# A list-scheduled megakernel: side work of the first mixer held behind its filter groups, and the end of an inverse moved one phase on

## The chip, the cores and the metric

The kernel is one program on one core of a Trainium2 chip. The core has five engines with queues of their own: TensorE (PE: matmuls, and PEld: its weight loads), VectorE (DVE), ScalarE (ACT), GpSimd (POOL) and SyncE (SP, which here only issues DMAs; ACT issues some as well). The metric is the device time of one execution in microseconds, lower is better. The kernel before took 4566.36 us (median of three runs, 4564.21 to 4567.75).

## What is computed

Eight sequences of 512 tokens with 256 channels go through four layers, each a mixer and a feed-forward part, all in float32: `x = x + layernorm(f(layernorm(x)))`, eight times. Only the first mixer matters here:

```python
q, k, v = silu(short_conv(x @ W.T))                  # 4 heads of 64
delta_out = delta_rule_chunkwise(q, k, v, beta)      # chunks: T = inverse(I - A), then a scan
local_s, local_m, local_l = fir(v, 3), fir(v, 15), fir(v, 63)
probs = softmax(logits / temp) * (1 - 5 * eps) + eps
o = (probs[0] * local_s + probs[1] * local_m + probs[2] * local_l
     + probs[3] * delta_out + probs[4] * v)
out = rmsnorm(o, norm_w) @ Wo.T
```

The reference uses chunks of 32 tokens; the kernel inverts 64 x 64 blocks, as two 32 x 32 ones and what lies between them.

## The kernel before

The program is written with a tile framework. Its planner orders the instructions of each engine itself: among those that it takes to be ready it issues the one written first. An instruction that it takes to be ready early can so land far ahead of work that was written before it. Once ordered, each engine's queue runs in that order. Pools of tiles that follow one another share an area of on-chip memory; what touches a later pool first waits for the earlier ones' last uses.

The function `l0_attn` has three phases:

1. **Front** (0 to about 241 us of the profile): `front(b)` for each of the 8 sequences: transposes, projections, short convolutions on DVE (L457), transposed values into `Vw`, products k k^T into `S`, all but `Vw` stored to DRAM (`S` to `l0s` at L506 and L510). After the fourth sequence `strengths(0)` and the DVE part of `inverse(0)` run between the steps.
2. **Filters** (248 to about 396 us): 32 groups g of 8 channels. `filters(g)` multiplies `Vw` with Toeplitz matrices `toep` (16 matmuls, L625) into one of 6 PSUM tiles, two per group; DVE multiplies by the gates `gt` into `pr` (L630; 2 buffers); POOL adds four terms to two (`s1`, L636, 1 buffer) and two to one (`s2`, L638, 2 buffers); ACT issues two stores of `s2` to `l0f` (L640). Three `toep` buffers are filled by two SP loads each (L542, L545), three groups ahead. Beside it, written between the groups: `gates(h)` (DVE with one ACT exponential, before g = 0 and at g = 4, 12, 20), `value_scales` (g = 2, an rsqrt on DVE), `scaled_v(b)` (every fourth group, L610, stored by ACT at L613), `query_scales` (g = 22), `strengths(1)` (g = 4), the end of `inverse(0)` with `load_tt` for two sequences (g = 1) and `inverse(1)` (g = 6 to 24, one step per group, its end as the last).
3. **Last phase** (419 to about 701 us): generators `back(b)`, two or three alive at a time and a new one every 16 steps, each some 32 us after the one before. `loads(b)` reads what phases 1 and 2 stored, one sequence ahead; at the end `load_x` reads the residual and `project_out` adds the result to it.

`inverse(g)` handles four sequences in half of the residual buffer `XA` (`X` in the profile): it loads 2 MB of `S` from DRAM (L331) and two small tiles, scales (L343), eliminates 30 columns on DVE (L351, L354), scales again (L357). Its end is `affine_select` on POOL (L360), a diagonal copy (L363), a 2 MB store by SP (L364), and four times a transposing ACT copy into one of two `tt` buffers (L367) with a 512 KB store issued by ACT (L368). `load_tt(b)` reads those blocks back, for sequences 0 and 1 into `XA`, after two POOL memsets (L398, L399). `inverse(0)` writes `XA` for sequences 0 to 3, `inverse(1)` for 4 to 7.

The order in which phase 2 is written ends so:

```python
if g == 6:
    inv = inverse(1)
if 6 <= g < 26:
    next(inv, None)
if g == 26:
    for _ in inv:
        pass
```

Of the kernel before, what the change touches and what calls it, by code (L numbers as in the profile page):

```python
# [19 lines left out]
P = 128  # L20
# [254 lines left out]
def l0_attn(K):  # L275
# [6 lines left out]
    with ExitStack() as es:  # L282
# [45 lines left out]
        def inverse(g):  # L328
# [42 lines left out]
            yield  # L371
# [35 lines left out]
        with ExitStack() as e1:  # L407
# [117 lines left out]
            with ExitStack() as ef:  # L525
# [4 lines left out]
                NB_T = 3  # L530
                toep = []
# [17 lines left out]
                rw_all = p1.tile([P, 24, 64], F32, name="rw_all")  # L549
                for r in range(2):  # L550
                    nc.sync.dma_start(
                        out=rw_all[64 * r:64 * r + 64].rearrange("p r t -> p (r t)"),
                        in_=rows_d[:, 256:28 * 64])
# [4 lines left out]
                def wide(name, n=256):  # L558
                    return p1.tile([P, n], F32, name="w" + name)
                gz = rw_all[:, 0:20, :].rearrange("p (h f) t -> p h f t", h=H)  # L560
                gm = wide("gm").rearrange("p (h t) -> p h t", h=H)
                gt = p1.tile([P, H, 4, 64], F32, name="gt")
# [23 lines left out]
                def query_scales():  # L586
                    ssq = wide("ssq")
# [28 lines left out]
                def filters(g):  # L616
# [18 lines left out]
                    s1 = p1.tile([P, 4, 2, 64], F32, tag="s1", name=f"s1_{g}")  # L635
# [9 lines left out]
                for g in range(G):  # L645
                    filters(g)
                    if g % 8 == 4 and g < 24:
                        gates(g // 8 + 1)
                    if g == 2:
                        value_scales()  # L650
                    if g == 22:
                        query_scales()
                    if g % 4 == 3:
                        scaled_v(g // 4)
                    if g == 1:
                        for _ in inv:
                            pass
                        for b in range(2):
                            load_tt(b)
                    if g == 4:  # L660
                        strengths(1, p1)
                    if g == 6:
                        inv = inverse(1)
                    if 6 <= g < 26:
                        next(inv, None)
                    if g == 26:
                        for _ in inv:
                            pass
# [62 lines left out]
        def back(b, TT, TS, qT, kT, V, F):  # L731
# [128 lines left out]
            K.load_x(K.i["x"], [b])  # L860
# [20 lines left out]
        live, done, begun, steps = [back(0, *ahead[0])], 0, 1, 0  # L881
        while live:
            for x in list(live):
                if next(x, x) is x:
                    live.remove(x)
            steps += 1
            if begun < NB and steps >= 16:
                live.append(back(begun, *ahead[begun]))
                begun, steps = begun + 1, 0
                if begun < NB:  # L890
                    ahead[begun] = loads(begun)
# [1739 lines left out]
```

## Time and profile before

The profiled execution took 4566.32 us, its span 4564.6 us.

| stretch of the span, us | what | length | PE busy | DVE busy | ACT busy | POOL busy |
|---|---|---|---|---|---|---|
| 201.0 to 241.0 | end of the front | 40.00 | 32.50 | 17.85 | 28.39 | 8.35 |
| 241.0 to 248.4 | until the last `S` store has landed | 7.40 | 0.00 | 0.00 | 0.66 | 0.00 |
| 248.4 to 395.9 | filters, to the end of the last `pr` | 147.50 | 120.86 | 128.23 | 6.79 | 80.69 |
| 395.9 to 411.4 | to the end of the last `s2` | 15.50 | 0.00 | 0.00 | 5.65 | 3.51 |
| 411.4 to 419.3 | to the first matmul of the last phase | 7.90 | 0.00 | 0.00 | 0.00 | 7.71 |
| 484.5 to 517.0 | one period of the last phase | 32.50 | 30.05 | 21.46 | 12.36 | 7.67 |

Busy times are of one engine each and overlap. "L360" is a line of the kernel; names are the program's tiles without their numbers. A queue such as SPq is the sequencer that issues DMAs: its rows are issues, and a transfer goes on after it. "A <- B: t" in a table of waits says that A stood idle for t until B released it. The end of `inverse(0)` is in the profile at 201.8 to 224.5 us, that of `inverse(1)` at 386.1 to 404.5 us.

### The profile page before, as it was taken

The numbers are of one execution on the slowest core, as the hardware profiler recorded it, in microseconds if no ns is written. First come the engines' busy times: TensorE is split into PE (matmuls) and PEld (weight loads), VectorE is DVE, ScalarE is ACT, GpSimd is POOL, SyncE is SP. The second block draws the span as 40 slices with busy tenths as digits, with TensorE's granted clock in tenths as the row PEclk, the third lists the DMA queues.
The fourth block names the chain that finished last, engine by engine and source line by source line (L and its number), as shares of the span: only waits on it lengthen the run. The fifth ranks groups of instructions, "written<-read, shape, count | busy, mean of one in ns | idle before, by whom it ended". The sixth has DMA issues, their size and how long they took to land. (4 is left out here: it accounts for less than half of the span.)

```text
span 4564.6 us, 63271 instructions
## 1 busy us (share of the span) xinstructions
PE 3962.3 (87%) x21672; PEld 2630.5 (58%) x21672; DVE 2697.3 (59%) x7151; ACT 1982.4 (43%) x4082; POOL 2123.0 (47%) x2079
## 2 busy tenths in 40 slices
PE   8876988999998599789999978898888876899997
PEld 3434775555655399644454544565655544678884
DVE  7775656456747611255566534888888899721115
ACT  5511333444344233334444444767676655311112
POOL 0044222444344244345555423889888879223321
PEclk9987998999999799889999988899999886899999
DMA  4477611000000199500000002344333434337653
GB/s 116 123 208 216 147 48 62 3 8 6 7 5 20 52 251 252 147 5 10 6 6 6 1 23 63 122 127 128 123 119 126 124 109 137 104 115 233 228 181 113
DMA packets 389361, 442.89 MB, mean 97 GB/s; under 512 B 147469, under 2 KB 271487, under 8 KB 388527
## 3 DMA queue, kind: packets, MB, share of 16 engines
q1 hardware_dynamic: 361087, 390.18, 28.6%
q0 software_dynamic: 16272, 31.87, 2.6%
q10 hardware_dynamic: 11680, 16.80, 1.1%
q8 instruction: 172, 2.82, 0.3%
q14 instruction: 150, 1.23, 0.1%
HBM read 372.49 MB, written 66.26 MB: 96 GB/s over the span
## 5 line engine op out<-in xcount | busy, mean ns | idle before, releaser
L2046 POOL TENSOR_TENSOR h<-h,C 128x1024 f32<-128x1024 f32 x256 | 614.0, 2412 | 134.8 <-DVE h L2042 92.9
L2042 DVE TENSOR_TENSOR_SCAN h<-dA,dB 128x512 f32<-128x512 f32 x480 | 568.3, 1209 | 90.9 <-ACT dA L2030 75.2
L1000 POOL TENSOR_SCALAR p<-p,rs 128x128 f32<-128x128 f32 (+3 forms) x256 | 276.6, 1089 | 418.1 <-DVE rs L999 258.9
L2030 ACT ACTIVATE dA<-dl,A 128x512 f32<-128x512 f32 x480 | 330.5, 690 | 174.4 <-DVE h L2042 173.7
L1566 DVE CUSTOM_DVE_ANT_0 junk<-S,mask 128x256 f32<-128x256 f32 (+3 forms) x512 | 249.5, 487 | 194.1 <-PE S L1560 155.8
L2059 PE MATMUL y<-C,h 128*128 128x128 f32 x2048 | 296.3, 296 | 68.4 <-POOL h L2046 68.2
L2059 PEld LDWEIGHTS y<-C,h 128*128 128x128 f32 x2048 | 261.9, 154 | 154.0 <-POOL h L2046 97.6
L1594 ACT ACTIVATE PT<-T 128x128 f32<-128x128 f32 (+3 forms) x512 | 198.2, 435 | 277.9 <-PE T L1589 273.9
L1560 PE MATMUL S<-KZ,QT 64*128 64x512 f32 (+3 forms) x1024 | 259.7, 490 | 23.6 <-DVE mx L1566 23.1
L2258 PE MATMUL gb<-xbT,w_b 128*128 128x256 f32 (+1 forms) x1472 | 255.3, 332 | 1.0 <-ACT ts L2462 0.6
L2258 PEld LDWEIGHTS gb<-xbT,w_b 128*128 128x128 f32 x1472 | 230.2, 191 | 23.1 <-ACT ts L2462 0.8
L2264 DVE TENSOR_TENSOR hTb<-sb,gb 128x512 f32<-128x512 f32 x71 | 48.8, 688 | 325.4 <-PE gb L2258 325.4
L1844 PE MATMUL pf<-fT,w_l_ffn 128*128 128x512 f32 x384 | 208.3, 681 | 30.1 <-ACT fT L1838 10.5
L2025 POOL TENSOR_TENSOR dB<-du,B 128x1024 f32<-128x1024 f32 x96 | 234.0, 2438 | 0.1
L1589 PE MATMUL T<-QT,KZ 64*128 64x384 f32 (+3 forms) x1024 | 216.7, 464 | 2.9 <-ACT PT L1594 2.5
L2025 DVE TENSOR_TENSOR dB<-du,pb 128x1024 f32<-128x1024 f32 x160 | 191.2, 1195 | 23.2 <-ACT pb L2023 21.3
L182 POOL TENSOR_TENSOR X<-X,yn 128x256 f32<-128x256 f32 (+1 forms) x56 | 79.5, 1439 | 257.1 <-ACT yn L177 227.1
L1334 ACT ACTIVATE hT<-h,w_l_ffn 128x128 f32<-128x128 f32 x384 | 109.8, 368 | 196.6 <-PE h L1329 196.6
L1329 PE MATMUL h<-xgT,w 128*128 128x128 f32 x1536 | 184.1, 278 | 0.0
L1597 POOL TENSOR_SCALAR_AFFINE_SELECT PT<-PT 128x512 f32<-128x512 f32 x128 | 81.5, 637 | 218.8 <-ACT PT L1594 206.0
L1560 PEld LDWEIGHTS S<-KZ,QT 64*128 64x128 f32 x1024 | 116.4, 192 | 114.1 <-issue 57.9
L2495 POOL DMA_INDIRECT ys<-yb,place x71 | 70.0, 986 | 238.5 <-ACT yb L2494 224.3
(601 smaller groups left out, 9238.1 us busy)
## 6 DMA issues: line engine op xcount, KB each, us to landing
w_b<-l3f_w SPq DMA_DIRECT2D x138, 512.0 KB
C<-xdd SPq DMA_DIRECT2D x256, 256.0 KB
B<-xdd SPq DMA_DIRECT2D x256, 256.0 KB
w<-l1f_w SPq DMA_DIRECT2D x48, 1024.0 KB
w<-l1f_w SPq DMA_DIRECT2D x48, 256.0 KB
toep<-l0fd SPq DMA_DIRECT2D x32, 320.0 KB
X<-x SPq DMA_DIRECT2D x16, 512.0 KB
toep<-l0fd SPq DMA_DIRECT2D x32, 256.0 KB
```

Of the source, the lines that this page charges most:

```text
L1000: nc.gpsimd.tensor_scalar(p[:, 0:n], p[:, 0:n], rs, None, ALU.mult)
L1560: nc.tensor.matmul(ps[:, 0:n], lhsT=QT[half, qt * P:n], rhs=KZ[half, j % 2, 0:n], start=True, stop=True)
L1566: nc.vector.tensor_tensor_reduce(out=junk[:, 0:n], in0=ps[:, 0:n], in1=mask[:, L - n:L], scale=1.0, scalar=-3.0e38, op0=ALU.add, op1=ALU.m ...
L1589: nc.tensor.matmul(ps[:, 0:n], lhsT=KZ[half, j % 2, kt * P:(kt + 1) * P], rhs=QT[half, kt * P:L], start=True, stop=True)
L1594: nc.scalar.activation(PT[:, j, :], ps[:, 0:n], AF.Exp)
L1844: nc.tensor.matmul(ps, lhsT=gu[:, k, j * 768 + c * P:j * 768 + (c + 1) * P], rhs=R[b]["fT"][:, k, :], start=(k == 0), stop=(k == 1))
L2025: on.tensor_tensor(dBs[k], R[b]["du", h], B[:, None, :].to_broadcast([P, 2, L]), ALU.mult)
L2030: nc.scalar.activation(dA, R[b]["dl", h][:, c, :], AF.Exp, scale=A[:, 2 * h + c, n:n + 1])
L2042: nc.vector.tensor_tensor_scan(hs[k][:, c, :], dA, dBs[k][:, c, :], 0.0, ALU.mult, ALU.add)
L2046: nc.gpsimd.tensor_tensor(hs[k], hs[k], row_C.pop(k)[:, None, :].to_broadcast([P, 2, L]), ALU.mult)
L2059: nc.tensor.matmul(R[b]["y", h][q // 2][:, q % 2, c * P:(c + 1) * P], lhsT=t[:, c, q * P:(q + 1) * P], rhs=K.ident, is_transpose=True, sta ...
L2258: nc.tensor.matmul(ps[:, q, :], lhsT=ww[:, k, (c + q) * P:(c + q + 1) * P], rhs=xT[:, k, :], start=(k == 0), stop=(k == 1))
```

## The change

- The yield at the end of `inverse` moves into the loop over q, so that each of the four copies with its store is a step of its own.
- `behind()` is new: what is written inside it on SP, DVE, ACT or POOL is queued behind the instruction written last on that engine (an edge of order, no wait for its end). All side work of group g stands in such a block after `filters(g)`.
- `inverse(1)` now takes one step at g >= 6 until its DVE part is through (18 steps, g = 23). Its end goes to the last phase: one step at every odd step of the second batch, each in a `behind()`. An assertion says that it is through before the fifth sequence's loads.
- `load_x` in `back` stands in a `behind()`.
- The tiles `s1`, `gt`, `gm`, `ssq` and `rw_all` are made before the `toep` tiles, in that order, and the load of `rw_all` is written before the `toep` memsets. `s1` is one tile instead of one per group from a single buffer.

```diff
@@ inverse(g)
                 nc.scalar.dma_start(
                     out=tt_d[g * P:(g + 1) * P, 1024 * q:1024 * q + 1024],
                     in_=tt.rearrange("p i j -> p (i j)"))
-            yield
+                yield
+
+        @contextmanager
+        def behind():
+
+            with ExitStack() as stack:
+                traced = nc.cur_bb.bb.instructions
+                for e in (mybir.EngineType.SP, mybir.EngineType.DVE,
+                          mybir.EngineType.Activation, mybir.EngineType.Pool):
+                    stack.enter_context(tc.issue_after(
+                        next(x for x in reversed(traced) if x.engine == e)))
+                yield
@@ filters
                 NB_T = 3
+                s1s = p1.tile([P, 4, 2, 64], F32, name="s1")
+                gt = p1.tile([P, H, 4, 64], F32, name="gt")
+                gm = p1.tile([P, 256], F32, name="wgm").rearrange("p (h t) -> p h t", h=H)
+                ssq = p1.tile([P, 256], F32, name="wssq")
+                rw_all = p1.tile([P, 24, 64], F32, name="rw_all")
+                for r in range(2):
+                    nc.sync.dma_start(
+                        out=rw_all[64 * r:64 * r + 64].rearrange("p r t -> p (r t)"),
+                        in_=rows_d[:, 256:28 * 64])
                 toep = []
...
-                    s1 = p1.tile([P, 4, 2, 64], F32, tag="s1", name=f"s1_{g}")
+                    s1 = s1s
...
                 for g in range(G):
                     filters(g)
-                    if g % 8 == 4 and g < 24:
-                        gates(g // 8 + 1)
...
+                    with behind():
+                        if g % 8 == 4 and g < 24:
+                            gates(g // 8 + 1)
+                        if g == 2:
+                            value_scales()
+                        if g == 22:
+                            query_scales()
+                        if g % 4 == 3:
+                            scaled_v(g // 4)
+                        if g == 1:
+                            for _ in inv:
+                                pass
+                            for b in range(2):
+                                load_tt(b)
+                        if g == 4:
+                            strengths(1, p1)
+                        if g == 6:
+                            inv, inverted = inverse(1), False
+                        if g >= 6:
+                            inverted = inverted or next(inv)
+                assert inverted
@@ back(b), and the loop of the last phase
-            K.load_x(K.i["x"], [b])
+            with behind():
+                K.load_x(K.i["x"], [b])
...
             steps += 1
+            if begun == 2 and steps % 2:
+                with behind():
+                    next(inv, None)
             if begun < NB and steps >= 16:
                 live.append(back(begun, *ahead[begun]))
                 begun, steps = begun + 1, 0
+                assert begun < HALF or next(inv, 0) == 0
                 if begun < NB:
                     ahead[begun] = loads(begun)
```

More of the change, by code (lines that the diff above doesn't have):

```diff
@@ L1 @@
 import math
-from contextlib import ExitStack
+from contextlib import ExitStack, contextmanager
 from itertools import chain
@@ L547, in load_toep @@
                         in_=window(fd, 3 * g * 1536 + 384, (8, 80), (1536, 2), (1, 512)))
[L549 to L553, printed above, removed]
                 for g in range(NB_T):
                     load_toep(g)
-                def wide(name, n=256):
-                    return p1.tile([P, n], F32, name="w" + name)
                 gz = rw_all[:, 0:20, :].rearrange("p (h f) t -> p h f t", h=H)
-                gm = wide("gm").rearrange("p (h t) -> p h t", h=H)
-                gt = p1.tile([P, H, 4, 64], F32, name="gt")
                 def gates(h):
@@ L586, in query_scales @@
                 def query_scales():
-                    ssq = wide("ssq")
                     nc.vector.tensor_scalar(
@@ L646, in l0_attn @@
                     filters(g)
-                    if g % 8 == 4 and g < 24:
-                        gates(g // 8 + 1)
[L649 to L668, printed above, removed]
+                    with behind():
[19 more added lines that the diff above has]
+                assert inverted
         p1, p2 = pool(es, "ba", 1), pool(es, "bb", 2)
@@ L880, in l0_attn @@
         ahead = {b: loads(b) for b in range(2)}
-        live, done, begun, steps = [back(0, *ahead[0])], 0, 1, 0
+        live, begun, steps = [back(0, *ahead[0])], 1, 0
         while live:
```

## The prediction

> **What bounds the kernel now.** Only the first mixer is touched, and it ends at about 701 us of a span of 4564.6 us, so I read that stretch alone. First the busy table by stretches (columns: length, then PE, PEld, DVE, ACT, POOL busy with counts, granted clock, DMA share, GB/s):
>
> ```profile
> 241.00:248.40 7.40, 0.00 (x0) 0.00 (x0) 0.00 (x0) 0.66 (x2) 0.00 (x0) 0.63 0.77 137
> 248.40:274.77 26.37, 11.93 (x48) 5.32 (x48) 21.12 (x43) 2.53 (x4) 5.52 (x3) 0.65 0.90 290
> 274.77:395.90 121.13, 108.93 (x464) 53.17 (x464) 107.11 (x171) 4.26 (x4) 75.17 (x63) 0.95 0.63 191
> 248.40:395.90 147.50, 120.86 (x512) 58.49 (x512) 128.23 (x212) 6.79 (x8) 80.69 (x66) 0.89 0.68 209
> 395.90:411.40 15.50, 0.00 (x0) 0.00 (x0) 0.00 (x0) 5.65 (x4) 3.51 (x4) 0.50 0.87 299
> 411.40:419.30 7.90, 0.00 (x1) 0.03 (x2) 0.00 (x0) 0.00 (x0) 7.71 (x15) 0.50 0.82 210
> ...
> 484.50:517.00 32.50, 30.05 (x394) 23.72 (x393) 21.46 (x61) 12.36 (x27) 7.67 (x4) 1.00 0.57 133
> ```
>
> The projections (front) end near 241, the filter loop runs from 248.4 to the last gated product at 395.9, the last phase starts at 419.3. In the loop DVE (128.23) is loaded more than PE (120.86): DVE is its floor. Between 395.9 and 419.3 PE does nothing. The last phase is nearly full of PE (30.05 of 32.50).
>
> Second, the waits of 240 to 420 (us in total, times, longest):
>
> ```profile
> PE pW L740 <- DMA TS<-l0s: 28.4, 1, 28.4
> ...
> PE pf L625 <- DMA l0v<-vs: 20.9, 1, 20.9
> ...
> POOL toep L534 <- DMA l0s<-S: 20.0, 1, 20.0
> POOL s L638 <- DMA l0f<-s: 16.6, 5, 6.3
> DVE rky L90 <- DMA l0s<-S: 12.3, 1, 12.3
> ```
>
> Third, the timeline, for what stands in each queue at the two idle places:
>
> ```profile
> 246.64 0.34 SPq L331 DMA_DIRECT2D X<-l0s  x1
> 248.35 1.13 SPq L551 DMA_DIRECT2D rw_all<-l0rows  x2
> 248.50 5.52 POOL L534 MEMSET toep<- 128x2048 f32 x3 [20.04 <-DMA l0s<-S]
> 248.85 1.53 DVE L90 TENSOR_SCALAR rky<-SSK 128x128 int32<-128x128 int32 x1 [12.27 <-DMA l0s<-S]
> ...
> 274.77 2.47 DVE L630 TENSOR_TENSOR pr<-pf,gt 128x512 f32<-128x512 f32 x4
> ```
>
> ```profile
> 386.06 4.07 POOL L360 TENSOR_SCALAR_AFFINE_SELECT X<-X 128x4096 f32<-128x4096 f32 x1
> ...
> 392.59 3.82 ACT L367 COPY tt<-X 128x1024 f32<-128x1024 f32 x2 [92.09 <-POOL X L363]
> ...
> 400.21 1.91 ACT L367 COPY tt<-X 128x1024 f32<-128x1024 f32 x1 [3.80 <-DMA l0tt<-tt]
> ...
> 404.49 2.11 SPq L74 DMA_DIRECT2D X<-x  x3
> ...
> 410.64 0.72 POOL L638 TENSOR_TENSOR s<-s 128x256 f32<-128x256 f32 x1 [6.27 <-DMA l0f<-s]
> ```
>
> At the head, side work runs before the filters that were written first: the 2 MB load X<-l0s, the rsqrt of value_scales and five scaled_v. So the first product `pr` comes at 274.77, though the loop's memory was free at 248.4. At the tail the end of inverse(1) stands in ACT's queue: copies that wait for their own stores, with the stores f<-s behind them. POOL's last s2 waits for those and ends at 411.36; only then is the loop's memory free for the last phase.
>
> **The change part by part.** The profiled execution took 4566.32 us (span 4564.6 and 1.7 around it); the median of the three runs is 4566.36, so one sum serves both. Against it:
>
> (a) The end of inverse(0) leaves the front. There it cost POOL 4.07 + 0.29 and four memsets of 0.95, ACT four copies of about 1.95 with four DMA issues, SP five issues, and 5 MB (2 MB t, 2 MB tt, 1 MB read back). PE was busy 32.50 us of 201 to 241. At the 94% of 100 to 150 us (46.92 of 50) the same work takes 34.6, which would save 5.4; the other end is 0, as the last front has no next one beside it. I take 3, and 1 more for the stores of S, which land at 248.4 with less traffic beside them. **-4.0** (0 to -6).
>
> (b) The loop. Behind-edges put gates(0) first on DVE. Loop memory frees at 244.4. rw_all (768 KB) and the first filter load (576 KB) take 1.34 MB / 290 GB/s = 4.6 us. One gates is 24.4 / 4 = 6.1 us of DVE by its rows, with an ACT table load of 1.28. So the first `pr` is at about +12 (the two gates in the trace took 265.59 to 274.79, 9.2, which would make it +13.8). What DVE then still has to do is all of 128.23 less gates(0) 6.1 and three filter copies 1.3: 120.8, at 95% busy (47.1 of 50 in 340 to 390) 127 us. PE, starting at about +7 (a memset of 1.9, then the loads) with 32 groups of 16 x 0.235 = 3.76, needs 120 and is done earlier. 12 + 127 = 139.
>
> (c) What the loop newly holds: the end of inverse(0) at g=1 with its 5 MB and its POOL, ACT and SP instructions, and X<-l0s at g=6 instead of ahead. Behind a late copy on ACT stand the f stores, behind those POOL's s2, s1, and then DVE's `pr`; behind a late issue on SP stand the filter loads that PE waits for. The nearest row is the same work at the tail, where POOL stood 16.6 us for f stores. Three groups of PSUM (3 x 3.76 = 11.3) lie between PE and DVE, two `pr` buffers before POOL, so I take 16.6 - 11.3 = 5. The ends are 0 (cover whole) and 34 (the whole chain as the front ran it, 201.8 to 236). The loop becomes 144 against 147.5: **-3.5** (-14 to +26: DVE at 100% and no stall, or the 34).
>
> In bytes: the loop moved 147.5 us x 209 GB/s = 30.8 MB; with 5 more in 144 us it is 249 GB/s, under the 290 seen at a share of 0.90. The Trainium skill, "DMA: Bandwidth & Descriptors", section "Issuing engines are not separate DMA queues", speaks against the change: transfers of SP and of ACT run on the same 16 engines and interleave, so ACT's tt stores delay SP's filter loads. If all 5 MB went ahead of the loads, at the page's roughly 358 GB/s (estimate) that is 14 us in place of my 5, and the total 9 us higher; the trace's share of 0.63 in the loop says that most of it fits beside.
>
> (d) Tail. From the last `pr` to the last s2 were 15.5 us; without copies ahead of the f stores it is s1 1.27 + s2 0.73 + hand-overs, 2.7 as at 275.5 to 278.2. **-12.8** (-13 to -6). New here: scaled_v(7) is held behind group 31, DVE 1.22 and a 512 KB store that must land before TS may be loaded: **+1.5** (0 to 4).
>
> (e) Start of the last phase, 7.9 us now. Three X<-x loads (1.5 MB, 5.3 us at 299 GB/s) no longer stand before it, partly drained by 411.4: **-2.5** (-5 to 0). They come back as one each behind the loads of their batch, as for the other batches now (issued 457.46, needed by POOL at 476.29): free, while those 18 us cover them.
>
> (f) The end of inverse(1) enters the last phase: POOL 4.4 in a gap of 11.2 before its next work, free; SP one issue; 4 MB where the share is 0.57, more than one 32.5 us period has free but with loads issued a period ahead, free if that holds; ACT four copies, 7.8, plus a possible wait for their stores of 3.8. ACT is busy 12.36 of 32.5 but feeds PE, which has 2.45 us idle a period. **+4** (0 to 11.6).
>
> (g) The order of tiles in memory: nothing. POOL, DVE and SP made their first use of the loop's memory, in three different tiles, within 0.5 us of each other when the same store had landed (248.35, 248.50, 248.85). So the whole area, not a tile, is waited for. If I misread that, filter memsets start at 241: -7.
>
> PE's idle before the last phase shrinks from 28.4 to about 12 us. The clock reads 0.63 over the 7.4 us of idle of 241 to 248.4 already, so no gain of clock is counted.
>
> Sum: -4.0 - 3.5 - 12.8 + 1.5 - 2.5 + 4 = -17.3: **4549 us**, own range 4537 to 4560.
>
> **The rivals.** Less than 0.2% (9.1 us) is no difference here.
> 1. The queues jam in the loop, ending slower. Place: ACT and SP between g=1 and g=8, where a queue in order stands on a piece that waits for its transfer. The end of inverse(0) takes the 34 us it took in the front, and X<-l0s another 2 MB / 209 GB/s = 10: 44 in place of 5, so 4588. It decides slower from 32 us of stall on. For it: SP stood 16.2 us for f stores in the loop already. Against: PSUM and two-deep buffers cover about 11 to 15 us, and the work lies 15 groups ahead of any need.
> 2. DVE is the floor anyway and a milder jam takes the gain: 17 us of stall in place of 5, or ACT's copies at 11.6 with 4 more in (c). 4561.
> 3. No jam at all: stalls 0, DVE at 100% (-6), copies in the last phase free: 4549 - 5 - 6 - 4 = 4534. With the layout effective, 4527.
> 4. The edges bind nothing: pieces are already behind. Excluded by the timeline: five scaled_v (written at g=3 to 19) stand before the first `pr`.
>
> **How the numbers follow.** Likeliest 0.53, rival 3 0.14, rival 2 0.18, rival 1 0.15. Faster 0.67, same 0.18, slower 0.15. The range leaves out rival 1 and the extreme of 3: 4530 to 4574.
>
> **What would show it.** First `pr` L630 near 256, not 274.77; no L610 before it; L367 copies in two sets of four, near 260 to 285 and 455 to 490, none at 206 to 224 or after the last `pr`; POOL's wait s L638 for l0f under 8 us; PE pW waiting about 12; last phase from about 398, as long as now plus 4. Wrong in (c) if PE pf waits for toep loads more than some 10 us or DVE shows idle between g=1 and g=8; wrong in (f) if the period after the second batch starts grows beyond 37; wrong in (g) if L534 starts before the S stores land.

## The result, and the profile after

The changed kernel takes **4580.57 us** (median of seven runs, 4579.56 to 4583.87) against 4566.36 (seven runs, 4564.21 to 4570.07): ratio 1.0032, 95% interval 1.0020 to 1.0044. It is 14.2 us slower; 4549 was forecast. The profiled execution has a span of 4578.8 us, 14.2 more than before.

The same busy table of stretches as before the change (length, then PE, PEld, DVE, ACT, POOL busy with counts, granted clock, DMA share, GB/s). The loop's memory now comes free at 244.10, the first `pr` starts at 257.21, the last ends at 414.06, the last `s2` at 417.11, the last phase's first matmul is at 427.84:

```profile
237.20:244.10 6.90, 0.00 (x0) 0.00 (x0) 0.00 (x0) 0.03 (x1) 0.01 (x1) 0.71 0.67 114
244.10:257.21 13.11, 4.25 (x19) 2.27 (x21) 8.92 (x13) 1.75 (x2) 5.56 (x3) 0.50 0.83 196
257.21:317.21 60.00, 37.25 (x158) 17.78 (x156) 38.53 (x59) 8.91 (x6) 29.07 (x26) 0.78 0.82 262
317.21:384.06 66.85, 57.53 (x244) 25.72 (x240) 64.76 (x106) 0.94 (x2) 33.08 (x26) 0.94 0.61 185
384.06:414.06 30.00, 22.82 (x96) 9.63 (x96) 22.02 (x37) 0.00 (x0) 18.61 (x16) 0.89 0.47 144
244.10:414.06 169.96, 121.85 (x512) 55.41 (x512) 134.22 (x213) 11.61 (x10) 86.32 (x71) 0.84 0.68 206
414.06:417.11 3.05, 0.00 (x0) 0.00 (x0) 1.13 (x2) 0.00 (x0) 2.83 (x2) 1.00 0.10 23
417.11:427.84 10.73, 0.00 (x1) 0.03 (x1) 0.00 (x0) 1.28 (x1) 7.84 (x16) 0.52 0.66 172
```

Three of the edits did what the diff says: the loop starts 4.4 us earlier, the first `pr` 17.6 us earlier, and 3.05 us instead of 15.5 lie between the last `pr` and the last `s2`. But the loop between them takes 169.96 us instead of 147.4. In its first 60 us after the first `pr` both engines that could bound it stand idle for more than a third of the time (busy: PE 37.25, DVE 38.53 of 60). Then DVE is full (64.76 of 66.85) while PE is not. In the last 30 us PE first stands another 8.4 us for DVE's `pr`; from 394.48 on it sets the pace, and DVE has 8 us to spare. The granted clock over the loop is lower than before (0.84, was 0.89), but that is not the cause: the 512 filter matmuls kept PE busy for 121.85 us, against 120.86.

Whom PE waited for (us in total, times, longest), first before the change (240 to 420 us), then after it (240 to 425 us):

```profile
PE pf L625 <- DMA toep<-l0fd: 1.6, 3, 0.7
```

```profile
PE pf L635 <- DMA toep<-l0fd: 39.5, 5, 16.7
PE pf L635 <- DVE pr L640: 15.8, 5, 4.6
```

The longest, 16.7, is the wait for the very first filters; 22.7 come after the first `pr` (0.4 before the change). What SP's queue had between the filter loads in that time:

```profile
268.15 0.33 SPq L562 DMA_DIRECT2D toep<-l0fd  x1
269.15 0.32 SPq L364 DMA_DIRECT2D l0t<-X  x1
269.52 0.42 SPq L565 DMA_DIRECT2D toep<-l0fd  x1
271.87 0.33 SPq L562 DMA_DIRECT2D toep<-l0fd  x1
276.80 0.32 SPq L565 DMA_DIRECT2D toep<-l0fd  x1
281.81 1.20 SPq L388 DMA_DIRECT2D rws<-l0rows  x2
283.95 0.34 SPq L562 DMA_DIRECT2D toep<-l0fd  x1
284.33 1.05 SPq L565 DMA_DIRECT2D toep<-l0fd  x1
287.31 6.75 SPq L413 DMA_DIRECT2D X<-l0tt  x4
296.53 4.64 SPq L399 DMA_DIRECT2D l0g<-bts  x4
301.48 0.34 SPq L562 DMA_DIRECT2D toep<-l0fd  x1
```

```profile
305.77 3.98 PE L635 MATMUL pf<-toep,Vw 128*64 128x256 f32 x16 [11.45 <-DMA toep<-l0fd]
```

A pair of filter loads (L562, L565) is due every 3.76 us, the PE time of a group. Here 17 us pass between the pair of 284 and that of 301. Between them stand the loads of `tt` for two sequences (1 MB) and the four g stores, and PE then stands 11.45 us for filters. The 2 MB of `t` went out on SP ahead of that (269.15), the 2 MB of `X` come in behind it (302.40), and ACT stores its 2 MB of `tt` between 271 and 284 us. Between 270 and 290 us the DMA engines are busy for 1.01 and 0.92 of the time.

The second half of the loop shows in DVE's rows, here from 358 us on:

```profile
358.59 2.29 DVE L620 TENSOR_TENSOR vs<-Vw,SSK 128x1024 f32<-128x1024 f32 x1
360.80 1.18 DVE L354 TENSOR_TENSOR X<-X,tmp 128x476 f32<-128x476 f32 x1
361.90 0.68 DVE L640 TENSOR_TENSOR pr<-pf,gt 128x512 f32<-128x512 f32 x1
...
364.21 1.55 DVE L576 TENSOR_TENSOR rw_all<-rw_all,w_l_attn 128x320 f32<-128x320 f32 x1
365.68 1.16 DVE L351 TENSOR_TENSOR tmp<-X 128x456 f32<-128x456 f32 x1
```

Here `scaled_v` (L620) and the last `gates` (L576 on) share DVE with the columns of `inverse(1)` (L351, L354), and no `pr` runs from 363.73 to 369.66. The columns begin behind the scaling at L343, first before the change, then after it:

```profile
302.91 3.08 DVE L343 TENSOR_TENSOR X<-X,gn 128x2048 f32<-128x2048 f32 x1
```

```profile
311.96 2.87 DVE L343 TENSOR_TENSOR X<-X,gn 128x2048 f32<-128x2048 f32 x1
```

Before the change, three `gates` and most of the fourth (reciprocals L577 at 272.19, twice, 296.20 and 302.45) and five of eight `scaled_v` were done by then. Now two `gates` (reciprocals at 334.50 and 371.89) and six `scaled_v` come after the columns have begun: about 11 and 5 us of DVE more than before in that stretch, at 6.1 and 1.7 us each.

Written as a sum, the loop is DVE's busy time plus its idle time. Busy went from 128.23 to 134.22 (+5.99), idle from 19.17 to 35.74 (+16.57): +22.56. Half of the 5.99 are the three copies into `toep`, which ran beside POOL's memsets and took 4.34 us in place of 1.31; the section on the hardware shows what else lengthens DVE's instructions.

### The profile page after: what moved, and what is told of

It is laid out like the page before. It is cut to its first block, busy times and chain, and to the rows that moved or that the text cites. A ratio compares the mean times of both kernels' runs of the same rounds, so it can differ in the third digit from the quotient of the medians.

```text
span 4578.8 us, 63269 instructions
## 1 busy us (share of the span) xinstructions
PE 3970.7 (87%) x21672; PEld 2630.5 (57%) x21672; DVE 2702.4 (59%) x7151; ACT 1983.0 (43%) x4082; POOL 2121.0 (46%) x2079
## 5 line engine op out<-in xcount | busy, mean ns | idle before, releaser
L2044 ACT ACTIVATE dA<-dl,A 128x512 f32<-128x512 f32 x480 | 330.5, 690 | 175.8 <-DVE h L2056 173.9
L1858 PE MATMUL pf<-fT,w_l_ffn 128*128 128x512 f32 x384 | 210.0, 686 | 26.1 <-ACT fT L1852 10.4
L2039 DVE TENSOR_TENSOR dB<-du,pb 128x1024 f32<-128x1024 f32 x160 | 191.1, 1195 | 22.7 <-ACT pb L2037 21.3
```

Of the source, the lines that this page charges most:

```text
L1858: nc.tensor.matmul(ps, lhsT=gu[:, k, j * 768 + c * P:j * 768 + (c + 1) * P], rhs=R[b]["fT"][:, k, :], start=(k == 0), stop=(k == 1))
L2039: on.tensor_tensor(dBs[k], R[b]["du", h], B[:, None, :].to_broadcast([P, 2, L]), ALU.mult)
L2044: nc.scalar.activation(dA, R[b]["dl", h][:, c, :], AF.Exp, scale=A[:, 2 * h + c, n:n + 1])
```

## The experiments

Two theories, with the letters of the texts on record. **Q** (A in the first texts): the held transfers stand in front of PE's filters. **D** (B in the first): the holds move DVE work out of the time in which DVE has nothing else into the time in which it is full. R and C are their rivals. The texts of e1 to e9 count PE's whole wait for `toep`, with 16 to 21 us for the first filters; the results below and the table at the end count from the first `pr` on. "The loop" runs from the first memset of `toep` to the end of the last `pr`. Loops and waits come from one profiled execution of each kernel; only the times and ratios have an interval.

**e1**, the end of `inverse(0)` and its `load_tt` not held:

```diff
@@ after.py, the loop over g
+                    if g == 1:          # ahead of "with behind():"
+                        for _ in inv:
+                            pass
+                        for b in range(2):
+                            load_tt(b)
```

> The changed kernel, but the end of inverse(0) and load_tt(0), load_tt(1), written at g = 1, are not held behind the filters. Theory A (the filter loop loses its 22 us because these 5 MB and their waiting issues stand in SP's and ACT's queues ahead of the filter loads): PE's wait for toep falls from 39.5 us to under 10, the loop from 170 us to about 145, the front gets its 4 us back, total about 4558. Rival B (the loop loses because held side work piles up on DVE late, where DVE is full from 368 to 396 while PE starves): the loop stays over 160 us and the total over 4572.

4578.92 us (ratio 1.0023, 1.0014 to 1.0032). The loop fell by 11.2 to 158.7 us, PE's wait for filters inside it from 22.7 to 14.4. Most of the rest is one place: `X<-l0s` and the g stores, which SP took 9.91 us to issue at 290. Both theories lost a number: the 5 MB are worth 11 us of the loop, but the loop is far from 145; and 4.1 of the 11.2 went back at its head, where the 5 MB stand again in the front and the memory comes free at 248.2.

**e2**, the end of `inverse(1)` kept in the loop, behind g = 24 and later:

```diff
-                            inverted = inverted or next(inv)
+                            next(inv, None)
@@ the loop of the last phase
-            if begun == 2 and steps % 2:
-                with behind():
-                    next(inv, None)
```

> The changed kernel, but the end of inverse(1) is held behind group 24 of the filter loop instead of in the last phase. If moving it is worth -12.8 + 4 as forecast, this is about 9 us slower than the changed kernel (4589). If seven groups of filters after it are enough to cover it, only the last phase changes, by the 2.7 us that it grew: 4578.

4584.80 us (1.0041, 1.0027 to 1.0055). The last `pr` ends at 421.5 instead of 414.1. Between the two expectations: by the two ratios the move to the last phase gains about 4 us, which their intervals do not tell from nothing.

**e3**, the loads of `load_tt` for sequences 0 and 1 issued by ACT instead of SP:

```diff
-                                load_tt(b)
+                                load_tt(b, nc.scalar)
```

> The changed kernel, but the loads of load_tt(0) and load_tt(1) are issued by ACT instead of SP; the same bytes at the same place. Theory A1 (order in SP's queue: the filter loads wait behind issues that wait): PE's wait for toep falls from 39.5 us to under 25 and POOL's wait for f stores grows instead, total about 4572. Rival C (the 16 DMA engines are full, so it doesn't matter which queue issues): PE's wait for toep stays within 5 us of 39.5 and the total within 4 us of 4580.

4583.21 us (1.0034, 1.0022 to 1.0046). PE waited 14.7 us for filters inside the loop, 8 less, and 22.0 for DVE, 6 more; the loop took 168.3. The time and the loop hardly change, so the queue that issues this 1 MB of the 5 hardly matters. A wait for filters of 31.1 us in all fits neither text (under 25, and within 5 of 39.5): what PE no longer waits for filters it waits for DVE.

**e4**, the kernel before with one part of the change alone: the end of `inverse(1)` in the last phase. Nothing in the loop is held and the layout is the old one (the new yield and `behind()` itself, as in the change, are not shown):

```diff
@@ before.py, the loop over g
-                    if 6 <= g < 26:
-                        next(inv, None)
-                    if g == 26:
-                        for _ in inv:
-                            pass
+                    if g >= 6:
+                        inverted = inverted or next(inv)
@@ the loop of the last phase
+            if begun == 2 and steps % 2:
+                with behind():
+                    next(inv, None)
```

> The kernel before with one part of the change alone: the end of inverse(1) goes to the last phase, held there; nothing is held in the filter loop, the layout is as before. By the terms of the prediction: tail -12.8, last phase +2.7 as measured in the changed kernel, total about 4556. Rival: other f stores or the loads of x fill the tail, total within 4 us of 4566.

4564.01 us (0.9992, 0.9983 to 1.0001). The loop took 143.2 us, the last phase started at 405.9 instead of 419.3 and took 280.1 instead of 274.7. A gain of the expected kind and less than half its size (4.2 us against 4568.23 on the same chip), at the edge of what can be told from nothing.

**e5**, side work not held on SP:

```diff
-                for e in (mybir.EngineType.SP, mybir.EngineType.DVE,
+                for e in (mybir.EngineType.DVE,
                           mybir.EngineType.Activation, mybir.EngineType.Pool):
```

> The changed kernel with one of the four queues not held: side work is held on DVE, ACT and POOL, not on SP. On SP that moves only the 2 MB load X<-l0s (ahead of the first filter load) and the two rws loads (ahead of the fourth group's filter loads); t store, load_tt, the four g stores and the gb load keep their places. Theory Q (filter loads stand in SP's queue behind held pieces that wait for data): those that wait longest are still there, so PE pf waits for toep 25 us or more (39.5 and 31.2 so far) and the time stays within 5 us of 4580. Theory D (DVE has no side work until X<-l0s and gb have come, about 312 us, and all of it afterwards): X is there from the start and the start of inverse(1) depends on gb alone, which comes some 8 us earlier, so DVE's idle time falls by about 8 and the loop from 170 to 162: 4572.

4585.75 us (1.0034, 1.0022 to 1.0046), the loop 170.0. D's 162 is missed. `X<-l0s` ahead of the first filters moved the first `pr` 4 us further from the start of the loop, and the wait for filters fell only to 16.7.

**e6**, `strengths(1)` and the first step of `inverse(1)` not held; **e7**, the same with e1:

```diff
+                    if g == 4:          # ahead of "with behind():"
+                        strengths(1, p1)
+                    if g == 6:
+                        inv, inverted = inverse(1), False
+                        next(inv)
```

> The changed kernel with strengths(1) and the first step of inverse(1) (X<-l0s, gb load, sign) not held; the end of inverse(0), load_tt and the rest stay held. The g stores then stand in SP's queue one group earlier, before load_tt. Theory Q: t store, load_tt and g stores still wait in front of filter loads: toep wait 20 to 31 us, loop 160 or more, 4570 or more. Theory D: DVE has inverse(1)'s columns from about 290 us on, idle under 10 us between 257 and 316, loop 150 to 155 and 4561 to 4566.

> Both together: the end of inverse(0) with load_tt, strengths(1) and the first step of inverse(1) not held; gates, value_scales, scaled_v, query_scales and the columns of inverse(1) held. In SP's queue only the rws loads, the g stores and the gb load are left between filter loads. Theories Q and D together (no late transfer in the loop): toep wait under 12 us, loop 150 or less of 248 to 398, time 4560 to 4566 (tail -12.5, late load of TS +2.8 and last phase +2.7 as before, loop 0 to +4). Rival R (the hold itself costs: held columns and scales stand on DVE in front of pr products wherever their data come from): toep wait falls, yet the loop stays over 157 and the time over 4573.

e6: 4597.18 us (1.0061, 1.0048 to 1.0075), loop 173.9. Theory D's number fell: the columns started at 311.1, no earlier than in the changed kernel, as `gb` still stood behind the held transfers. Q's wait of 20 to 31 us was missed too: 43.9. e7: 4575.38 (1.0015, 1.0006 to 1.0024), loop 154.1; the loop lies between the two texts, the time where R has it. In e7 PE is fed (3.0 us of wait for filters), and yet the loop is 6.7 us longer than before the change. Its stretches from the first `pr`, then the whole loop:

```profile
266.50:326.50 60.00, 59.14 (x256) 29.22 (x254) 53.40 (x94) 0.94 (x2) 31.94 (x28) 1.00 0.71 213
326.50:372.60 46.10, 34.57 (x148) 16.21 (x144) 46.10 (x80) 0.47 (x1) 23.34 (x19) 0.92 0.61 180
372.60:402.60 30.00, 23.57 (x96) 10.00 (x96) 19.03 (x28) 0.00 (x0) 17.06 (x16) 0.83 0.43 130
248.50:402.60 154.10, 121.62 (x512) 57.84 (x512) 127.46 (x213) 3.58 (x6) 77.88 (x65) 0.89 0.65 191
```

PE is full for 60 us, then DVE for 46 without a gap, and PE loses 11.5 us there; at the end DVE idles for 11 us. That is what D says, with next to nothing left of Q.

**e8**, the filter loads of g = 3 to 31 issued by POOL:

```diff
-                        load_toep(g + NB_T)
+                        load_toep(g + NB_T, nc.gpsimd)
```

> The changed kernel, but the filter loads of groups 3 to 31 (58 issues) are issued by POOL and not by SP; all holds as they are. Theory Q: SP's queue can no longer stand between PE and its filters: PE pf waits for toep under 10 us in place of 39.5, and what is left is DVE's; time 4560 to 4570. Theory D: PE's wait for toep only moves into a wait for DVE, total within 5 of 4580. What an issue costs on POOL no row shows; POOL was busy 80 of 147 us in the loop, so from about 1 us an issue on POOL itself becomes the bound, and then the run says nothing on either (the time would be well over 4590).

4587.41 us (1.0043, 1.0029 to 1.0056), and it settles nothing on Q: on POOL the loads stood behind `s1` and the held pieces as well (POOL waited 21.7 us for PE at L562), and DVE's busy time in the loop rose from 134.2 to 148.7.

**e9**, every hold kept, side work behind earlier groups; **e10**, the same on e7:

```diff
-                        if g % 8 == 4 and g < 24:
-                            gates(g // 8 + 1)
-                        if g == 2:
+                        if g in (0, 3, 5):
+                            gates((g + 3) // 3 if g < 5 else 3)
+                        if g == 1:
                             value_scales()
-                        if g == 22:
+                        if g == 7:
                             query_scales()
-                        if g % 4 == 3:
-                            scaled_v(g // 4)
+                        if 2 <= g < 10:
+                            scaled_v(g - 2)
```

> The changed kernel, every hold kept, but the side work that needs nothing late is held behind earlier groups: gates(1), (2), (3) behind g = 0, 3, 5 (were 4, 12, 20), value_scales behind 1 (2), scaled_v(b) behind 2 + b (4b + 3), query_scales behind 7 (22). No instruction is added or taken away, and SP's and ACT's order of loads and copies stays. Theory D (the holds move DVE work out of the time in which DVE has nothing else into the stretch where it is the bound): DVE was idle 21.5 us in the first 60 us after the first pr and full in the 67 after; gates(2), gates(3), query_scales and six scaled_v, some 28 us of DVE by their rows, ran after 310 us. At least half of the idle time is filled, and PE no longer paces the end (8 us idle on DVE there): the loop falls from 170 to about 150 to 157, the time to 4561 to 4568; the v store of scaled_v(7) no longer delays TS (another 2 to 3). Theory Q (PE lacks filters because SP stands still): the toep wait of 39.5 us is untouched, so the loop stays within 5 us of 170, the time within 5 of 4580 less the 3 of TS.

> e7 (end of inverse(0), strengths(1) and first step of inverse(1) not held) with the side work held behind the earlier groups as in e9. e7's loop took 154.1 us: DVE busy 127.5, idle 9.1 before the first pr, 6.6 in the 60 us after, 11.0 in the last 30. Theory D: the last part falls to about 4 and the middle one by 3: loop 144 to 147, with TS 2 to 3 us earlier: 4563 to 4566. Theory R (the order edges as such cost, whatever stands behind them): loop stays over 151 and the time over 4571.

e9: 4572.57 us (1.0008, 0.9999 to 1.0017), loop 161.0. Nothing but the place of side work of DVE, with the stores that depend on it, differs from the changed kernel, and 8 us are gone. e10: 4565.00 (0.9995, 0.9986 to 1.0004), loop 149.9. First the 60 us after e9's first `pr` and its last 30, then the same of e10:

```profile
259.30:319.30 60.00, 33.55 (x142) 15.91 (x138) 58.37 (x95) 10.04 (x8) 31.77 (x26) 0.81 0.88 286
...
376.40:406.40 30.00, 29.24 (x126) 14.46 (x122) 23.43 (x35) 0.00 (x0) 17.72 (x16) 1.00 0.51 155
```

```profile
267.30:327.30 60.00, 47.33 (x202) 21.15 (x200) 59.48 (x108) 1.42 (x3) 30.79 (x21) 0.88 0.65 203
...
369.40:399.40 30.00, 29.22 (x126) 14.45 (x122) 22.47 (x34) 0.00 (x0) 17.59 (x16) 1.00 0.54 155
```

DVE's idle time in the 60 us after the first `pr` went from 21.5 us to 1.6 in e9, and from e7's 6.6 to 0.5 in e10. The profile puts only 8.1 us of PE's waits in e9's loop down to `toep`, but three more (12.5, 6.1 and 3.7 us) down to DVE rows (`vs` L620, `X` L343 and L354) on which the filter matmuls do not depend. The longest ends at 309.49, after a filter load that SP issued at 305.28, behind the `tt` loads and the g stores; so these are likely waits for filters too, as Q has it, and DVE now does side work meanwhile. Both loops lie above their ranges, by 4 and 3 us: in e10 the packed side work now keeps PE waiting at the start (12.6 us for DVE's `pr`), and PE's 29.2 of 30 at the end of both show that PE had work left over.

**e11** and **e13**, `strengths(1)` and the first step of `inverse(1)` written behind an early group, on e10. In e11 the free end of `inverse(0)` was written just ahead of the held block, so SP's edge was tied to a `load_tt` that had gone early, and `X<-l0s` stood in front after all (at 247.57). e13 writes it behind the block:

```diff
                     with behind():
+                        if g == 0:      # e11: g == 1
+                            strengths(1, p1)
+                            inv1 = inverse(1)
+                            next(inv1)
...
+                    if g == 1:          # e13: behind the block, e11: ahead of it
+                        for _ in inv:
+                            pass
+                        for b in range(2):
+                            load_tt(b)
+                        inv, inverted = inv1, False
```

> e10 with strengths(1) and the first step of inverse(1) written behind g = 1 (held) and not at 4 and 6: X<-l0s no longer stands before rw_all in SP's queue, and gb comes about three groups earlier, so the columns of inverse(1) can begin about 285 us and not 298. Theory D: first pr 13 us after the loop's memory is free (18 in e7), one more gain of 3 to 5 us on e10: 4559 to 4562. Theory Q: g stores and gb that wait stand in front of filter loads again: toep wait over 15 us, time over 4570.

> e11 with its order mended: the free end of inverse(0) and load_tt are written after the held block, so that X<-l0s and strengths(1) are really held behind filter loads (behind g = 0), and do not stand in front of rw_all. Theory D and my step (b): first pr 13 to 14 us after the loop's memory is free (18.5 in e11), the loop 144 to 146 in place of 149.6, time 4559 to 4562, which would be below the kernel before by more than 0.1%. Theory Q: X<-l0s (2 MB) and the g stores then stand in front of the filter loads of the fifth group: toep wait inside the loop over 8 us and nothing gained.

e11: 4564.82 us (0.9997, 0.9988 to 1.0006), first `pr` 18.5 us after the memory came free. e13: 4563.89 (0.9993, 0.9984 to 1.0002), first `pr` after 13.6 us, loop 145.4, with 9.4 us of PE's wait for filters, 8.2 of them behind `X<-l0s` and the g stores. The loop came out as D had it, the time 2 us above its range; the wait that Q named came too.

**e12**, the kernel before with the new layout alone:

```diff
@@ before.py, filters
+                s1s = p1.tile([P, 4, 2, 64], F32, name="s1")
+                gt = p1.tile([P, H, 4, 64], F32, name="gt")
...
                 toep = []
...
-                    s1 = p1.tile([P, 4, 2, 64], F32, tag="s1", name=f"s1_{g}")
+                    s1 = s1s
```

> The kernel before with the new layout alone: s1, gt, gm, ssq and rw_all made ahead of the toep tiles, rw_all's load written before their memsets, s1 one tile. My step (g): nothing, within 2 us of the kernel before on the same chip; the memset of toep still starts when the last S store has landed. If the layout were effective it would start some 7 us earlier and the time fall by up to 7; if it costs (DVE's copies into toep took 1.50 us each beside POOL's memsets in the changed kernel and 0.44 before), the time rises by up to 3.

4568.38 us (1.0001, 0.9992 to 1.0010), loop 148.1. POOL's first memset:

```profile
247.73 5.52 POOL L543 MEMSET toep<- 128x2048 f32 x3 [20.03 <-DMA l0s<-S]
```

It waits for the last store of S as ever. The layout does nothing.

**e14**, e13 with five stores of 1 MB that nothing waits for and that wait for nothing late (extra work, no part of the result):

```diff
+                        if g == 2:
+                            for b in range(5):
+                                nc.sync.dma_start(
+                                    out=spare_d[b * P:(b + 1) * P, :],
+                                    in_=Vw[:, b].rearrange("p j d -> p (j d)"))
```

> e13 with five more stores of 1 MB each (Vw to a spare DRAM tensor that nothing reads), issued by SP behind g = 2, all of whose data are there: as much traffic as the end of inverse(0) has, at the same place, with nothing to wait for. If the traffic itself starves PE: 5 MB at about 300 to 378 GB/s (the rate of 270 to 290 us in the changed kernel) are 13 to 17 us in front of the next filter loads; less two to three groups of filters in hand (3.76 us each) PE waits 4 to 9 us for toep in the loop and the loop grows by as much. If what counted was queues standing behind pieces that wait: the wait for toep stays under 2 us and the loop within 2 us of e13. e1 against the changed kernel took 11.2 us off the loop; whatever e14 adds is the part of it that is traffic.

4572.62 us (1.0010, 1.0001 to 1.0019), loop 156.9: 11.5 us more than e13. SP's rows, and PE's waits inside the loop:

```profile
281.12 15.33 SPq L673 DMA_DIRECT2D l0spare<-Vw  x5
296.84 0.32 SPq L563 DMA_DIRECT2D toep<-l0fd  x1
```

```profile
PE pf L636 <- DMA toep<-l0fd: 27.3, 3, 16.2
```

Five issues took SP 15.33 us, 342 GB/s for 5.24 MB, and the next filter load came behind them. So transfers that wait for nothing late suffice to starve PE: a queue need not stand behind a piece that waits for its data. The 11.5 us are close to the 11.2 that e1 took away; both are more than the 4 to 9 that the text on record gave to traffic.

**e15** and **e16**, e13 with side work spread over the groups:

```diff
-                        if g in (0, 3, 5):
-                            gates((g + 3) // 3 if g < 5 else 3)
+                        if g in (0, 2, 4):
+                            gates(g // 2 + 1)
-                        if g == 7:
+                        if g == 4:      # e16: g == 29
                             query_scales()
-                        if 2 <= g < 10:
-                            scaled_v(g - 2)
+                        if 22 <= g < 30:
+                            scaled_v(g - 22)
```

> e13 with its side work spread over the groups in which DVE has time: a group needs 3.76 us of PE and 1.36 of DVE for its pr, so 2.4 us a group are free, and the columns of inverse(1) use them up from g = 6 to 23. So gates(1), (2), (3) behind g = 0, 2, 4, value_scales behind 1, query_scales behind 4, scaled_v(b) behind 22 + b. e13 had PE idle for 14 of the first 60 us after the first pr, DVE full there. DVE part of the cause: about 10 us of DVE (scaled_v) leave that stretch and find room after 370, the loop falls from 145.4 to 138 to 141; the time to 4556 to 4560, a ratio of about 0.998. If PE's filters are the limit there (toep wait 9.4 in e13), the loop stays at 143 to 146 and the time within 3 of e13.

> As e15, but query_scales behind g = 29. DVE part of the cause: early stretch lighter by another 6 us, but some 20 small instructions stand between the last pr products, with three groups of PSUM (11 us) of cover, and query_scales' end may come after the last pr: loop 137 to 142, 0 to 3 us more between the last pr and the last phase: 4556 to 4562.

4565.60 us (0.9996, 0.9987 to 1.0005) and 4574.54 (1.0012, 1.0003 to 1.0021). Both missed. e15's loop is 148.9 us. The profile puts 1.8 us of PE's waits down to filters, and 8.6 more to a DVE row of `value_scales` on which the matmuls do not depend; that one comes behind `X<-l0s` and the g stores, like the 8.2 us of e13, so e15 most likely waits for filters as e13 does. What differs is DVE: its busy time in the loop rose to 137.0 us, against 126.5 in e13. Of these 10.5 us, 6.4 are work that e13 does only after its last `pr` (the last columns of `inverse(1)`: 204 DVE instructions in e13's loop, 213 in e15's). For the other 4 the section on the hardware has the likely reason. e16's loop is 155.1 us in its profiled execution, the slowest of its eleven (4581.60). `query_scales` ran on until after the last `pr`; SP stood for it (15.0 us for DVE at L607), and the last phase's first load went out at 411.70, 3.7 us after the last `s2`.

The table (profiled executions; PE's wait from the first `pr` on; DVE's idle time before the first `pr`, in the 60 us after it, between, and in the last 30):

| kernel | median, us | loop | PE waits for `toep` | DVE busy | DVE idle |
|---|---|---|---|---|---|
| before | 4566.36 | 147.4 | 0.4 | 128.2 | 5.2 + 8.0 + 2.5 + 3.5 |
| after | 4580.57 | 170.0 | 22.7 | 134.2 | 4.2 + 21.5 + 2.1 + 8.0 |
| e7: end of `inverse(0)`, start of `inverse(1)` free | 4575.38 | 154.1 | 3.0 | 127.5 | 9.1 + 6.6 + 0 + 11.0 |
| e9: side work earlier | 4572.57 | 161.0 | 8.1, likely more | 132.5 | 4.9 + 1.6 + 15.4 + 6.6 |
| e10: both | 4565.00 | 149.9 | 2.1 | 126.3 | 8.9 + 0.5 + 6.7 + 7.5 |
| e13: e10, start of `inverse(1)` held early | 4563.89 | 145.4 | 9.4 | 126.5 | 4.7 + 1.5 + 5.0 + 7.7 |
| e4: `inverse(1)`'s end alone | 4564.01 | 143.2 | 2.8 | 123.3 | 5.3 + 8.4 + 2.6 + 3.6 |

The four of after, e7, e9 and e10 show the cause: held transfers in the loop cost 15.9 us of it with late side work and 11.1 with early; side work held late costs 9.0 with the transfers and 4.2 without. With neither, 2.5 of the 22.6 us are left.

Two things limit these numbers. In e9, e10 and e13 the last columns of `inverse(1)` and its scaling (L357 at 410.8, 404.2 and 402.9 us) come after the last `pr`, 6.4 to 6.8 us of DVE that the loops of after and e7 contain (L357 at 391.5 and 371.7). No run tells how much of the 9.0 and 4.2 is that; after its first 60 us DVE had 22.0 us idle in e9's loop and 14.2 in e10's, more than these columns need. And in time the two parts weigh differently: by the ratios, side work held late costs some 11 us with the transfers and 9 without, the transfers some 8 and 6, since each ratio holds the front and the tail as well. Each of these four is good to 6 or 7 us only.

No kernel was shown faster than the one before: e4 and e13 are the nearest, and their intervals reach to 1.0001 and 1.0002.

## Why the prediction was wrong, step by step

From 4549 to 4580.57 are 31.6 us; 26.1 of them are the loop.

- **(a) end of `inverse(0)` out of the front: right.** S lands at 244.1 instead of 248.5: -4.4, forecast -4.0. In e2, e3, e8 and e9, which have the same front, the loop's memory comes free at 244.9 to 246.4, so part of the agreement is luck.
- **(b) the loop without its stalls: wrong.** The head came as forecast (first `pr` at +13.1; 12 and at most 13.8 were given). What failed is "What DVE then still has to do is all of 128.23 less gates(0) 6.1 and three filter copies 1.3: 120.8, at 95% busy": it took DVE's work as one sum that can be done at any time. (The row it cites, 47.1 of 50, is 94%, which would give 128 us; that is not the error.) Before the change 21.12 us of it filled the 26.27 us before the first `pr`; the holds moved such work beside the columns of `inverse(1)`. e9 puts that work early again: 9.0 us of loop, 8.0 of time. No kernel here reached the 139 us of this step; e4, which holds nothing in the loop, took 143.2, and e13 145.4. Rival 4 came close: it named the five early `scaled_v` as proof that the edges bind something, but their new place was not priced.
- **(c) the held end of `inverse(0)`: the mechanism was named, its size was not.** The term was 16.6 - 11.3 = 5 us of stall. Inside the loop PE waited 22.7 us for filters, and the transfers cost 11.1 to 15.9 us of loop. The check in bytes (249 GB/s on average, under 290) misled: between 270 and 290 us the rate was 378 and 304 GB/s with the DMA engines full, and an average over 144 us says nothing about 13 us in front of a load that is due in 11. The page weighed in the prediction (the Trainium skill, "DMA: Bandwidth & Descriptors", section "Issuing engines are not separate DMA queues") was right here: e3 shows no gain from another issuing engine. The 14 us that the prediction estimated from the page's rate for 5 MB stand beside 15.33 measured in e14.
- **(d) the tail: right, but for one term.** Last `pr` to last `s2` 3.05 us instead of 15.5: -12.45, forecast -12.8. But the store of `scaled_v(7)`, +1.5 in the sum, went out on ACT at 418.34 behind 8.31 us of `f` stores, and SP held the load of `TS` until 423.83 (4.9 us of waiting for `l0v<-vs`). With **(e)** the start of the last phase was forecast at 6.9 us and took 10.73: 3.8 too little. In e9 and e10, where `scaled_v(7)` is early, the last `s2` to the first matmul took about 8.8 and 8.9. The -2.5 for the three `X<-x` loads never appeared: even those are longer than the 7.9 of before.
- **(f) the end of `inverse(1)` in the last phase: right.** First matmul to the load at L221, 274.7 us before, 277.4 after: +2.7, forecast +4; e4 shows +5.3.
- **(g) the layout: right**, nothing (e12).
- **After the first mixer** the span shows 3.0 us more, forecast 0. From L221 to the end it took 3870.6 us before, 3873.6 after, 3871.2 in e1, 3876.1 in e7, 3868.7 in e10: no cause was found, and the spread holds both signs, up to 3883.1 in e16.

**Rivals.** Rival 1 (the queues jam) has the place and the sign, but its stall of 44 us is too long; rival 2 comes near the stall with its 17 us and has, with 4561, the wrong time, because the DVE side came on top. The rule "It decides slower from 32 us of stall on" counted stall alone. "Wrong in (c) if PE pf waits for toep loads more than some 10 us or DVE shows idle between g=1 and g=8" is what happened, both.

## What to carry to other kernels

Holding side work behind the piece beside which it is written is free only where the engine has time at that place: find the engine that is full there, and ask which of its idle time the work filled before. Price a moved transfer by the bytes that land in front of the next load on which the loop waits, at the peak rate, against the loads in hand, and not by the average rate of the stage. Where a stage is bounded by two engines in turn, draw up busy and idle time of both by quarters, before and after the move.

## What the runs showed of the hardware

In these runs a DVE instruction with two SBUF inputs and a POOL `tensor_tensor` hold each other up, and both show it as a longer duration. `scaled_v` on DVE takes 1.16 us with POOL idle (e13), and 2.29 when it starts inside POOL's `s1` (e15); the `s2` that comes meanwhile on POOL takes 1.59 us instead of 0.73. First e13, then e15:

```profile
287.77 1.16 DVE L620 TENSOR_TENSOR vs<-Vw,SSK 128x1024 f32<-128x1024 f32 x1
```

```profile
371.88 1.40 POOL L646 TENSOR_TENSOR s<-pr 128x512 f32<-128x512 f32 x1 [2.19 <-DVE pr L640]
372.08 2.29 DVE L620 TENSOR_TENSOR vs<-Vw,SSK 128x1024 f32<-128x1024 f32 x1
373.37 1.59 POOL L648 TENSOR_TENSOR s<-s 128x256 f32<-128x256 f32 x1
```

The DVE row begins at 372.08 and ends about 1.1 us after POOL's `s1` has ended at 373.28, which is its own length; `s2` then ends 0.6 us after DVE. The `pr` products, with one input in PSUM, keep a median of 678 to 691 ns in every run. The Trainium skill states such a lock ("SBUF — State Buffer", section "SBUF: two separate sides": the port pair that DVE and GpSimd share is an exclusive lock, and the one that starts first has it for its whole instruction). The runs agree, and e15 hints at its price for a schedule: its eight `scaled_v` have a median of 2292 ns, in e13 1216, and some 4 us of DVE's longer busy time in e15's loop are left when the work that e13 does after its last `pr` is taken off.

An issue on SP can stand until an earlier transfer lands with which it shares no data: the profile of the changed kernel puts 4.9 us of waiting at L562 down to `X<-l0s` and 4.5 us at L565 down to `l0t<-X`. And the time of an issue is not set by its bytes: the five 1 MB stores of e14 took 3.07 us each, a load of 2 MB, `X<-l0s`, 0.42 in e13. Whether what was issued ahead of them or their shape makes the difference, no run shows.
